# Cross-attention kernel: the first context, Wk, Wk_ip and x loads as one row on one DMA queue, in place of halves on two queues

## The chip, the cores and the metric

The kernel runs on one core of one Trainium2 chip. The metric is the device time of one execution in microseconds (us), the median of several runs. All data is float32.

## The reference, cut to what matters

`x` is (2, 2048, 640), `ctx_2048` is (2, 154, 1024). The 154 context rows are 77 text rows and 77 image rows, each with its own keys and values; there are 20 heads of 32.

```python
text, ip = ctx[:, :77], ctx[:, 77:]
q        = split_heads(x @ Wq.T)                       # 640 -> 20 heads x 32
k, v     = split_heads(text @ Wk.T), split_heads(text @ Wv.T)          # 1024 -> 640
k_ip, v_ip = split_heads(ip @ Wk_ip.T), split_heads(ip @ Wv_ip.T)
out = softmax(q k^T / sqrt(32)) v + softmax(q k_ip^T / sqrt(32)) v_ip
result = merge_heads(out) @ Wo.T + bo + x
```

## The kernel before, in words

All matrices lie transposed in HBM, the contracted dimension first. The 640 channels are cut into 5 chunks of 128 (`NC`), the 1024 context channels into 8 (`NCC`), and each batch's 2048 tokens into 4 blocks of 512 (`NHB`). A unit of work is a pair of a channel chunk (four heads) and half of the tokens; for each unit TensorE (PE) computes queries and scores, ScalarE (ACT), VectorE (DVE) and GpSimd (POOL) do the softmax, and PE applies it to the values. The order of everything behind the start is written out by hand in the string `SCHEDULE`; each engine works through its own instructions in that order. The change touches only what stands ahead of that string, the start of the program:

- Five small matmuls on zeros (line 576).
- The first queries, for chunks 0 of two units, from x's first block: lines 580 and 207. They need the five slices of x's first block (`xs[0]`, 128 channels by 512 tokens each; the first is loaded as two halves) and the first two column chunks of Wq (`wq_first`, which lies in the tile `aT`).
- The first two key projections, `project_kv(0)` (text, Wk) and `project_kv(1)` (image, Wk_ip), line 145. Each has eight steps, over the context chunks `k`. They need the context (`cT`, which lies in the tile `wo_ct`) and one 128-column slice of Wk and of Wk_ip (`load_w`, line 130; the slots lie in `aT`).
- Then `SCHEDULE` begins: the queries of x's second block (`q.0.1`, line 207, from `xs[1]`), the first scores (line 243), queries from x's third block, the first value projections (line 145 again, Wv and Wv_ip), and so on.

The transfers are issued from two queues: SyncE's (SP) and ScalarE's (ACT), `queues = nc.sync, nc.scalar`. ACT issues its transfers in line with its other work. Ahead of the loads that the change touches stand, split over both queues, x's first block and Wq's first two column chunks. Then, before:

```python
    for n, queue in enumerate(queues):
        load_ctx(n * half, queue)                       # context chunks 0-3 on SP, 4-7 on ACT
    for t in range(2):
        for n, queue in enumerate(queues):
            load_w(t, queue, slice(n * half, (n + 1) * half))   # Wk, then Wk_ip: rows of 0-3 on SP, 4-7 on ACT
    for k in range(NC):
        load_x(queues[k % 2])                           # x's second block: slices 0, 2, 4 on SP, 1, 3 on ACT
```

Behind these, all on SP: Wq's third column chunk (line 564), x's third block, Wv, Wv_ip, x's fourth block, the bias.

In the built program each transfer signals one of eight completion semaphores (DMAHW0 to DMAHW7), given out in turn over both queues together. A transfer is issued only when the transfer that last had its semaphore has landed, and the queue's later transfers wait behind it; so at most eight are under way.

Of the kernel before, what the change touches and what calls it, by code (L numbers as in the profile page):

```python
# [20 lines left out]
def kernel(  # L21
# [25 lines left out]
    nc = tc.nc  # L47
    P = 128
    NC = C // P
    NCC = CC // P  # L50
# [76 lines left out]
    wlist = [(src, c) for c in range(NC) for src in (WkT, WkipT, WvT, WvipT)]  # L127
    loaded = {}

    def load_w(n, queue=nc.sync, ks=slice(0, NCC)):  # L130

        src, c = wlist[n]
        w = wslots[n % len(wslots)]
        rows = src[ks.start * P : ks.stop * P, ts(c, P)]
        queue.dma_start(out=w[:, ks], in_=rows.rearrange("(k p) o -> p k o", p=P))
        loaded[n] = w

    def keys_in(ps):
# [33 lines left out]
    def load_x(queue=nc.sync):  # L172

        if slices:
            i, k = slices.pop(0)
            queue.dma_start(out=xs[i][:, k], in_=xT[ts(k, P), ts(i, TB)])
# [358 lines left out]
    queues = nc.sync, nc.scalar  # L535
    slices.pop(0)

    def load_first(queue, k, c, m=3):
        queue.dma_start(  # L539
            out=wq_first[:, k, c:m].rearrange("p c o -> p (c o)"), in_=WqT[ts(k, P), c * P : m * P]  # L540
        )

    half = NCC // 2

    def load_ctx(k, queue):
        queue.dma_start(
            out=wo_ct[:, ds(k * B * LT, half * B * LT)].rearrange("p (k n) -> p k n", k=half),
            in_=ctxT[ds(k * P, half * P), :].rearrange("(k p) n -> p k n", p=P),
        )
# [4 lines left out]
    for k in range(1, NC):  # L554
        load_x(queues[1 - k % 2])
        load_first(queues[k % 2], k, 0, 2)
    for n, queue in enumerate(queues):
        load_ctx(n * half, queue)
    for t in range(2):
        for n, queue in enumerate(queues):  # L560
            load_w(t, queue, slice(n * half, (n + 1) * half))
    for k in range(NC):
        load_x(queues[k % 2])
    nc.sync.dma_start(out=wq_first[:, :, 2], in_=WqT[:, ts(2, P)].rearrange("(k p) o -> p k o", p=P))
    for _ in range(NC):
        load_x()
    load_w(2)
    load_w(3)
    for _ in range(NC):
        load_x()  # L570
# [235 lines left out]
    for c, stages in enumerate(chains_of):  # L806
        for _, text in stages:
            for _, t in terms(text):
                for h in range(NH):
                    o = int(t[0]), NH * int(t[1]) + h  # L810
# [128 lines left out]
```

## Time and profile before

| | us |
|---|---|
| median of 3 runs | 496.41 (496.37 to 497.61) |
| profiled execution, its time | 499.75 |
| profiled execution, span from first to last instruction | 497.9 |
| PE busy in the span | 491.0 (99%) |
| DVE busy | 414.0 (83%) |
| POOL busy | 370.5 (74%) |
| ACT busy | 309.5 (62%) |

A profile is of one execution; its times count from the start of the span. In its rows "SPq" and "ACTq" are the instructions that issue transfers, q1 is SP's queue and q10 is ACT's. In a row of the timeline the first number is the start, the second the duration of all that the row merges, xN the number of instructions, and in brackets stands the idle time ahead of it and what ended it. A float32 matmul of the code shows as two PE instructions, so a key projection of eight steps is x16. PEclk is the share of the full TensorE clock that was granted. "Landing" is the time from a transfer's issue to its completion.

### The profile page before, as it was taken

To read this page: it belongs to the slowest core of one execution; us is meant where nothing else is said; L and a number is where in the kernel's file an instruction comes from. 1 tells how busy PE (TensorE), PEld (TensorE's weight loads), DVE (VectorE), ACT (ScalarE), POOL (GpSimd) and SP (SyncE) were. 2 spreads that over 40 slices of the span, in tenths; PEclk is the share of its full clock that TensorE was granted. 3 is DMA by queue.
4 is the path that set the end of the run, shared out by engine and by line. 5 is a ranking of instruction groups with operands and counts; after the bars stand their busy time and mean duration, and the time that the engine had idled before them with its cause. 6 is when DMAs were issued, how large, how long until landed. Compare 5 with 4: busy or idle time off the path is not lost.

```text
span 497.9 us, 10488 instructions
## 1 busy us (share of the span) xinstructions
PE 491.0 (99%) x4116; PEld 289.5 (58%) x4116; DVE 414.0 (83%) x416; ACT 309.5 (62%) x1002; POOL 370.5 (74%) x158
## 2 busy tenths in 40 slices
PE   9899999999999999999999999999999999999997
PEld 5666648548457547446566654754655685444443
DVE  0049999998899989979987996777789898999996
ACT  0266678978686778768899787577889862100000
POOL 0049988998988988978995768476589899798700
PEclk9899999999999999999999999999999999999999
DMA  8993044402341544696460667446551212320125
GB/s 285 302 311 90 10 130 116 130 2 74 82 149 44 168 135 132 211 393 198 113 223 18 182 213 240 136 142 204 187 145 42 87 45 85 128 84 2 42 84 211
DMA packets 67137, 69.38 MB, mean 139 GB/s; under 512 B 5520, under 2 KB 47120, under 8 KB 67088
## 3 DMA queue, kind: packets, MB, share of 16 engines
q1 hardware_dynamic: 64208, 65.86, 42.4%
q10 hardware_dynamic: 2880, 2.86, 1.8%
q8 instruction: 32, 0.52, 0.4%
q14 instruction: 17, 0.14, 0.1%
HBM read 54.94 MB, written 10.49 MB: 131 GB/s over the span
## 4 chain that ended last, share of the span: by engine, by line
PE 96%; DMA 3%; ACTq 0%; ACT 0%; DVE 0%; issue 0%; DVEq 0%
PE bank L207 34%; PE bank L890 11%; PE bank L342 11%; PE bank L243 10%; PE bank L500 10%; PE bank L145 9%; PE bank L481 7%; PE bank L510 3%; DMA aT<-in_L_xattn_Wk_dram 2%; DMA x<-in_x_dram 1%; ACTq L539 0%; ACT pb L255 0%; ACTq L553 0%; DVE acc L833 0%; DVEq L934 0%
## 5 line engine op out<-in xcount | busy, mean ns | idle before, releaser
L326 POOL TENSOR_TENSOR pb<-pb,rden 128x1848 f32<-128x1848 f32 (+1 forms) x60 | 176.0, 2943 | 30.4 <-DVE rden L321 23.9
L305 POOL TENSOR_TENSOR pb<-pb,mx 128x1848 f32<-128x1848 f32 (+1 forms) x39 | 121.5, 3128 | 58.7 <-DVE mx L291 58.5
L207 PE MATMUL bank<-x,wq 128*128 128x512 f32 x280 | 125.4, 598 | 0.1
L333 DVE STREAM_TRANSPOSE pb<-pb 128x1920 f32<-128x1920 f32 (+1 forms) x60 | 115.9, 1938 | 9.1 <-POOL pb L326 8.9
L291 DVE TENSOR_REDUCE mx<-pb 128x24 f32<-128x1848 f32 (+1 forms) x50 | 91.6, 1844 | 35.4 <-ACT pb L255 35.2
L255 ACT COPY pb<-bank 128x462 f32<-128x462 f32 (+1 forms) x200 | 85.4, 543 | 29.3 <-PE bank L243 28.9
L316 DVE TENSOR_REDUCE den<-pb 128x24 f32<-128x1848 f32 (+1 forms) x47 | 88.9, 1895 | 15.6 <-ACT pb L311 12.7
L207 PEld LDWEIGHTS bank<-x,wq 128*128 128x128 f32 x280 | 51.7, 190 | 60.0 <-issue 58.8
L311 ACT ACTIVATE pb<-pb 128x1848 f32<-128x1848 f32 (+1 forms) x39 | 65.6, 1684 | 17.5 <-POOL pb L305 17.4
L279 ACT ACTIVATE pb<-bank,mx 128x77 f32<-128x77 f32 x208 | 60.4, 388 | 6.5 <-DVE mx L294 6.5
L279 ACT ACTIVATE pb<-pb,mx 128x77 f32<-128x77 f32 x184 | 54.2, 355 | 1.9 <-DVE mx L291 1.8
L342 PE MATMUL bank<-pb,v 32*32 32x512 f32 x1600 | 55.2, 597 | 0.0
L207 PE MATMUL bank<-x,aT 128*128 128x512 f32 x116 | 52.0, 597 | 0.0
L145 PE MATMUL bank<-wo_ct,aT 128*128 128x154 f32 x320 | 47.4, 303 | 2.1 <-DMA aT<-in_L_xattn_Wk_dram 2.1
L243 PEld LDWEIGHTS bank<-kT,qT 32*128 32x128 f32 x1024 | 36.1, 184 | 21.6 <-issue 13.2
L145 PEld LDWEIGHTS bank<-wo_ct,aT 128*128 128x128 f32 x320 | 44.7, 194 | 5.8 <-issue 5.1
L243 PE MATMUL bank<-kT,qT 32*128 32x154 f32 x1024 | 45.1, 305 | 0.0
L279 ACT ACTIVATION_READ_ACCUMULATOR pb<-bank,mx 128x1 f32 x168 | 44.1, 268 | 0.0
L342 PEld LDWEIGHTS bank<-pb,v 32*32 32x32 f32 x1600 | 28.9, 103 | 22.7 <-issue 10.1
L481 PE MATMUL bank<-aT,wo_ct 128*128 128x512 f32 x80 | 36.3, 595 | 0.0
L207 PEld LDWEIGHTS bank<-x,aT 128*128 128x128 f32 x116 | 21.4, 191 | 24.1 <-issue 23.7
L500 PE MATMUL bank<-aT,wo_ct 128*128 128x256 f32 x128 | 32.2, 386 | 0.0
(83 smaller groups left out, 511.9 us busy)
## 6 DMA issues: line engine op xcount, KB each, us to landing
x<-in_x_dram SPq DMA_DIRECT2D x20, 1280.0 KB, 7.0
out_dram<-acc SPq DMA_DIRECT2D x19, 256.0 KB, 2.6
acc<-in_x_dram SPq DMA_DIRECT2D x16, 256.0 KB, 5.0
x<-in_x_dram SPq DMA_DIRECT2D x15, 256.0 KB, 5.7
out_dram<-x SPq DMA_DIRECT2D x15, 256.0 KB, 2.1
v<-vS SPq DMA_DIRECT2D x160, 20.0 KB, 2.9
aT<-in_L_xattn_Wv_dram SPq DMA_DIRECT2D x5, 512.0 KB, 5.7
aT<-in_L_xattn_Wv_ip_dram SPq DMA_DIRECT2D x5, 512.0 KB, 4.2
```

Source lines behind the costliest of these rows:

```text
L145: nc.tensor.matmul(keys_in(out), loaded[n][:, k, :], cT[:, k, :, t, :], start=(k == 0), stop=(k == NCC - 1))
L207: nc.tensor.matmul(pq, weight_of(q)[:, k, :], xs[place_of(u, h)][:, k, :], start=(k == 0), stop=(k == NC - 1), skip_group_check=loose,)
L243: nc.tensor.matmul(ps[g][:, ts(t, 2 * L)], qTs[(u, h)][g * D : (g + 1) * D, ts(st, P)], kT[g * D : (g + 1) * D, c, b].rearrange("p t l -> ...
L255: nc.scalar.copy(keys_of(u, s)[:, :, g], ps[g][:, : n * 2 * L].rearrange("p (n l) -> p n l", n=n))
L279: nc.scalar.activation(row, row if ps is None else rows_in(ps[g], n)[:, t, x], AF.Exp, bias=maxs[(u, s)][:, *one], accum_out=None if den i ...
L291: nc.vector.tensor_reduce(mx, rows_of(u, s), AX.X, ALU.max, negate=negate)
L305: nc.gpsimd.tensor_tensor(rows_of(u, s), rows_of(u, s), maxs[(u, s)].unsqueeze(3).to_broadcast([P, n, 2, L]), ALU.subtract)
L316: nc.vector.tensor_reduce(den_of(u, s), rows_of(u, s), AX.X, ALU.add)
L326: nc.gpsimd.tensor_tensor(rows_of(u, s), rows_of(u, s), rdens[(u, s)].unsqueeze(3).to_broadcast([P, n, 2, L]), ALU.mult)
L333: nc.vector.transpose(p, p)
L342: nc.tensor.matmul(pa[r][g * D : (g + 1) * D, :], v4s[q % 2][rows, g, k, :], zones[rows, :, g, k, :], start=(k == 0), stop=(k == NK - 1),)
L500: nc.tensor.matmul(part, w_of[m][:, kp, op], t_of(m, b, i)[:, kp], start=(op == kp == 0 and m in (1, 2, 5)), stop=(op == 1 and kp == 1 and ...
```

## The change

The context still comes in two halves, but Wk and Wk_ip come whole, and all of these and the five slices of x's second block are issued by SP, in this order: context chunks 0-3, Wk, context chunks 4-7, Wk_ip, x slices 0 to 4. ACT issues nothing behind x's first block and Wq. What is computed, and the order of it on PE, DVE and POOL, is the same.

```diff
-    def load_w(n, queue=nc.sync, ks=slice(0, NCC)):
+    def load_w(n):
 
         src, c = wlist[n]
         w = wslots[n % len(wslots)]
-        rows = src[ks.start * P : ks.stop * P, ts(c, P)]
-        queue.dma_start(out=w[:, ks], in_=rows.rearrange("(k p) o -> p k o", p=P))
+        nc.sync.dma_start(out=w, in_=src[:, ts(c, P)].rearrange("(k p) o -> p k o", p=P))
         loaded[n] = w
...
-    def load_ctx(k, queue):
-        queue.dma_start(
+    def load_ctx(k):
+        nc.sync.dma_start(
...
-    for n, queue in enumerate(queues):
-        load_ctx(n * half, queue)
-    for t in range(2):
-        for n, queue in enumerate(queues):
-            load_w(t, queue, slice(n * half, (n + 1) * half))
-    for k in range(NC):
-        load_x(queues[k % 2])
+    for k in (0, half):
+        load_ctx(k)
+        load_w(k // half)
+    for _ in range(NC):
+        load_x()
     nc.sync.dma_start(out=wq_first[:, :, 2], in_=WqT[:, ts(2, P)].rearrange("(k p) o -> p k o", p=P))
```

SP, behind its part of x's first block and Wq, before (`wo_ct` holds the context, `aT` the weights, `x_83` is x's second block):

```order
L546 DMA wo_ct<-in_ctx_dram 128x4x308 [waits DMAHW3_49]
L135 DMA aT<-in_L_xattn_Wk_dram 128x4x128 [waits DMAHW5_49]
L135 DMA aT<-in_L_xattn_Wk_ip_dram 128x4x128 [waits DMAHW7_49]
L176 DMA x_83<-in_x_dram 128x512 [waits DMAHW1_49]
L176 DMA x_83<-in_x_dram 128x512 [waits DMAHW3_49]
L176 DMA x_83<-in_x_dram 128x512 [waits DMAHW5_49]
L564 DMA aT<-in_L_xattn_Wq_dram 128x5x128 [waits DMAHW6_49]
```

SP at the same place in the changed kernel (its line numbers are up to three lower):

```order
L545 DMA wo_ct<-in_ctx_dram 128x4x308 [waits DMAHW3_49]
L134 DMA aT<-in_L_xattn_Wk_dram 128x8x128 [waits DMAHW4_49]
L545 DMA wo_ct<-in_ctx_dram 128x4x308 [waits DMAHW5_49]
L134 DMA aT<-in_L_xattn_Wk_ip_dram 128x8x128 [waits DMAHW6_49]
L175 DMA x_83<-in_x_dram 128x512 [waits DMAHW7_49]
L175 DMA x_83<-in_x_dram 128x512 [waits DMAHW0_49]
L175 DMA x_83<-in_x_dram 128x512 [waits DMAHW1_49]
L175 DMA x_83<-in_x_dram 128x512 [waits DMAHW2_49]
L175 DMA x_83<-in_x_dram 128x512 [waits DMAHW3_49]
L561 DMA aT<-in_L_xattn_Wq_dram 128x5x128 [waits DMAHW4_49]
```

Wk's transfer now reuses semaphore 4, which Wq's second slice had on ACT, and Wq's third column chunk reuses that of Wk itself, where it reused that of ACT's half of Wk.

ACT from its last transfer of x's first block on, before:

```order
L176 DMA x_82<-in_x_dram 128x512 [waits DMAHW2_49]
L546 DMA wo_ct<-in_ctx_dram 128x4x308 [waits DMAHW4_49]
L135 DMA aT<-in_L_xattn_Wk_dram 128x4x128 [waits DMAHW6_49]
L135 DMA aT<-in_L_xattn_Wk_ip_dram 128x4x128 [waits DMAHW0_49]
L176 DMA x_83<-in_x_dram 128x512 [waits DMAHW2_49]
L176 DMA x_83<-in_x_dram 128x512 [waits DMAHW4_49]
L221 ACT_TABLE_LOAD
L221 ACTIVATE qT_0_153<-bank_71 128x512 [waits PE_49]
L221 ACTIVATE aT<-bank_72 128x512 [waits PE_49]
```

And in the changed kernel:

```order
L175 DMA x_82<-in_x_dram 128x512 [waits DMAHW2_49]
L220 ACT_TABLE_LOAD
L220 ACTIVATE qT_0_151<-bank_71 128x512 [waits PE_49]
L220 ACTIVATE aT<-bank_72 128x512 [waits PE_49]
L590 COPY kT<-bank_69 128x77 [waits PE_49]
```

Five transfers leave ACT, and the load of its function table follows directly on x's first block.

PE at the two key projections and the start of `q.0.1`, before:

```order
L145 MATMUL bank_69<-wo_ct,aT 128x154 [waits DMAHW5_49,DMAHW3_49]
L145 MATMUL bank_69<-wo_ct,aT 128x154 x3
L145 MATMUL bank_69<-wo_ct,aT 128x154 [waits DMAHW6_49,DMAHW4_49]
L145 MATMUL bank_74<-wo_ct,aT 128x154 [waits DMAHW7_49]
L145 MATMUL bank_74<-wo_ct,aT 128x154 [waits DMAHW0_49]
L207 MATMUL bank_72<-x_83,aT 128x512 [waits DMAHW1_49,Activation_49]
```

And in the changed kernel:

```order
L144 MATMUL bank_69<-wo_ct,aT 128x154 [waits DMAHW4_49,DMAHW3_49]
L144 MATMUL bank_69<-wo_ct,aT 128x154 x3
L144 MATMUL bank_69<-wo_ct,aT 128x154 [waits DMAHW5_49]
L144 MATMUL bank_74<-wo_ct,aT 128x154 [waits DMAHW6_49]
L144 MATMUL bank_74<-wo_ct,aT 128x154 x7
L206 MATMUL bank_72<-x_83,aT 128x512 [waits DMAHW7_49,Activation_49]
```

PE's work is the same; the first step of each projection now waits for the whole of its weights, the fifth step of the first one for the second half of the context alone.

## Prediction

> **What bounds the kernel now.** First the page: shares, the slices of the span, the chain of waits.
>
> ```profile
> span 497.9 us, 10488 instructions
> ...
> PE 491.0 (99%) x4116; PEld 289.5 (58%) x4116; DVE 414.0 (83%) x416; ACT 309.5 (62%) x1002; POOL 370.5 (74%) x158
> ...
> PEclk9899999999999999999999999999999999999999
> ...
> PE 96%; DMA 3%; ACTq 0%; ACT 0%; DVE 0%; issue 0%; DVEq 0%
> ```
>
> PE is busy for 99% of the span and is 96% of the chain that ends it. The only other share of weight is DMA's 3%, and the only slices in which PE's clock is below nine tenths lie at the start (the second digit, 12 to 25 us). So I read the chain's first 40 us in order of time (start, duration, what):
>
> ```profile
> 2.14 5.79 DMA x<-in_x_dram
> ...
> 7.95 9.53 DMA aT<-in_L_xattn_Wk_dram
> ...
> 17.61 5.06 PE bank L145 x24
> 22.67 4.29 PE bank L207 x10
> ...
> 28.75 4.49 PE bank L207 x10
> ...
> 33.97 4.41 PE bank L145 x32
> ```
>
> and PE's own timeline at that place, and the granted clock around it (stretch, then length, busy time of PE, PEld, DVE, ACT and POOL, then PEclk, DMA share, GB/s):
>
> ```profile
> 14.34 1.22 PE L145 MATMUL bank<-wo_ct,aT 128*128 128x154 f32 x8
> 17.61 5.06 PE L145 MATMUL bank<-wo_ct,aT 128*128 128x154 f32 x24 [2.06 <-DMA aT<-in_L_xattn_Wk_dram]
> ```
> ```profile
> 14.50:17.50 3.00, 1.05 (x8) 0.82 (x7) 0.00 (x0) 2.08 (x3) 0.00 (x0) 1.00 1.11 354
> 17.50:18.00 0.50, 0.39 (x2) 0.42 (x3) 0.00 (x0) 0.29 (x1) 0.00 (x0) 0.79 0.98 353
> 18.00:21.00 3.00, 3.00 (x14) 3.00 (x13) 0.00 (x0) 0.35 (x2) 0.00 (x0) 0.50 0.85 264
> 21.00:21.50 0.50, 0.50 (x5) 0.50 (x4) 0.00 (x0) 0.00 (x0) 0.00 (x0) 0.80 0.80 143
> ```
>
> PE does four steps of the first key projection (8 instructions), then stands 2.06 us until ACT's half of Wk, issued at 7.95, lands at 7.95 + 9.53 = 17.48. Behind the wait it runs at half clock: 0.21 of the 0.5 us to 18.0, all 3.0 us to 21.0, 0.2 us after that, 3.41 us in all. PE's list of waits (us, times, longest) has nothing else but its start, so what it loses here moves everything behind it:
>
> ```profile
> PE bank L145 <- DMA aT<-in_L_xattn_Wk_dram: 2.1, 1, 2.1
> PE bank L576 <- DVE pb L574: 1.0, 1, 1.0
> ```
>
> **The change part by part.** *The stall and its clock.* The 24 instructions behind the wait took 5.06 us; the 32 of the first value projections take 4.41, so 24 at full clock are 24 x 4.41/32 = 3.31 us. The slow clock costs 5.06 - 3.31 = 1.75 us (half of 3.41 us of half clock is 1.71, the same). Stall and clock together are 2.06 + 1.75 = **3.81 us**; that is what there is to gain. The Trainium skill's TensorE: Matmul & The Clock Gate (What's actually happening) lets the clock fall after an idle window of about 3.4 us; by that rule a 2.06 us stall would cost itself alone, and the sum would be 2.06. The row says 0.50 behind a stall of 2.06, so the measurement decides, and I keep 1.75.
>
> *Why Wk is late.* These are issues on ACT, from its last slice of x's first block on, with its table load and its second copy of queries, and on SP:
>
> ```profile
> 5.20 0.33 ACTq L176 DMA_DIRECT2D x<-in_x_dram  x1
> 7.15 0.39 ACTq L546 DMA_DIRECT2D wo_ct<-in_ctx_dram  x1
> 7.95 0.38 ACTq L135 DMA_DIRECT2D aT<-in_L_xattn_Wk_dram  x1
> 8.67 0.43 ACTq L135 DMA_DIRECT2D aT<-in_L_xattn_Wk_ip_dram  x1
> ...
> 15.41 1.28 ACT L221 ACT_TABLE_LOAD   x1 [15.41 <-DMA aT<-in_L_xattn_Wk_dram]
> ...
> 17.20 0.59 ACT L221 ACTIVATE aT<-bank 128x512 f32<-128x512 f32 x1
> ```
> ```profile
> 5.00 0.39 SPq L546 DMA_DIRECT2D wo_ct<-in_ctx_dram  x1
> ...
> 8.30 4.46 SPq L176 DMA_DIRECT2D x<-in_x_dram  x3
> 17.49 0.38 SPq L564 DMA_DIRECT2D aT<-in_L_xattn_Wq_dram  x1
> ...
> 21.07 0.63 SPq L135 DMA_DIRECT2D aT<-in_L_xattn_Wv_ip_dram  x1
> ```
>
> While ACT's Wk waits its turn, SP's slices of x's second block, not needed before 22.67, move. From 16.0 to 17.5 us, the last stretch before the landing, the queues carried (packets, MB):
>
> ```profile
> q1 hardware_dynamic: 245, 0.45, 83.2%
> q10 hardware_dynamic: 90, 0.12, 22.5%
> ```
>
> 0.45 MB of x on q1 against 0.12 MB of weights on q10. The change puts x behind both weights on one queue. Whether that suffices is a sum of bytes.
>
> *When the loads land.* In MB: x's first block and Wq's two chunks are 1280 + 640 KB = 1.97, a half of the context 0.63, Wk 0.52, Wk_ip 0.52, a slice of x 0.26. In a row they end at 2.60 (context, first half), 3.12 (Wk), 3.75 (second half), 4.28 (Wk_ip), 4.54 (x's slice 0), 5.59 (slice 4). Up to 9.0 us the trace moved (and up to 28.0, for the lag below):
>
> ```profile
> DMA packets 1917, 2.37 MB, mean 263 GB/s; under 512 B 171, under 2 KB 1421, under 8 KB 1917
> ```
> ```profile
> DMA packets 8848, 8.28 MB, mean 296 GB/s; under 512 B 470, under 2 KB 7029, under 8 KB 8848
> ```
>
> Up to there both kernels move almost the same. For the rates I take windows of the trace, the second of them mostly Wv and Wv_ip, which have Wk's form, on SP's queue alone, the third x alone:
>
> ```profile
> 9.00:13.00 4.00, 4.00 (x10) 1.71 (x9) 0.00 (x0) 0.00 (x0) 0.00 (x0) 1.00 1.11 339
> 25.50:27.50 2.00, 2.00 (x20) 0.99 (x22) 0.00 (x0) 0.50 (x1) 0.00 (x0) 1.00 1.21 302
> 28.50:30.00 1.50, 1.50 (x11) 0.69 (x6) 0.10 (x1) 1.50 (x5) 0.00 (x0) 1.00 1.03 370
> ```
>
> Context at 339 GB/s, weights at 302, x at 370: the context's first half is through at 9.0 + 0.23/0.339 = 9.7, Wk at 11.4, the second half at 13.3, Wk_ip at 15.0, x's slices from 15.7 to 18.5. A landing comes later than the bytes:
>
> ```profile
> wo_ct<-in_ctx_dram SPq DMA_DIRECT2D x1, 616.0 KB, 6.6
> ...
> aT<-in_L_xattn_Wv_ip_dram SPq DMA_DIRECT2D x1, 512.0 KB, 8.2
> ```
>
> The context half issued at 5.00 landed at 11.6, its last byte being the 2.60th MB, moved at 9.7: 1.9 us. Wv_ip, issued at 21.07, landed at 29.3; all that stands ahead of it and itself are 8.27 MB, moved at 28.0: 1.3 us. With 1.3 to 1.9 the landings are Wk 12.7 to 13.3, context's second half 14.6 to 15.2, **Wk_ip 16.3 to 16.9**, x's slices 17.0 to 17.6 and then up to 20.4.
>
> *When PE wants them.* It comes to the first projection at 14.34 as now, to its fifth step at 14.34 + 8 x 0.138 = 15.44, to Wk_ip at 16.55, to x's second block at 18.75 and to its last slice 3.4 us later. Wk has 1.0 us to spare or more, the context 0.2 or more, x over 1.1. Wk_ip is a draw: PE waits for 0 to 0.4 us. I take 0.2, the middle, and no slow clock for it: the only stall of the trace with the clock recorded behind it is ten times as long. Gain 3.81 - 0.2 = 3.6; the ends are 3.8 and, with a wait of 0.4, 3.4.
>
> *What else moves.* SP issues nine transfers where it had six, three more at some 0.43 us; at 9.0 there are 4.28 - 2.37 = 1.9 MB queued ahead of the first x slice, and Wq's third chunk, held until 17.49 by ACT's half of Wk, now waits for Wk alone, 13 or so. Wk itself is issued at 7.15, when Wq's second slice on ACT lands (ACT's context half waits for the same there), 2.5 us before its first byte is due; without that cover each 0.4 us would count in full. SP can also be held behind two 512 KB loads:
>
> ```profile
> L176 SPq DMA_DIRECT2D x<-in_x_dram x5: 430/430/3990, 21.8 to 27.2; - x5
> ```
>
> An x slice right behind Wv and Wv_ip took 3.99 us to issue. The same at 8.4 ends at 12.4, still 2.6 us before its bytes are due. Loads for later (x's third block, due at 28.75 - 3.8) start no later than now, since SP stood from 12.8 to 17.49 there. ACT's table load moves from 15.41 to the time after its last issue at 5.2, and the copies of the first queries with it; PE needs the bank they free at 18.75, and at 17.8, where the second copy ends now, it would be in time. Worth nothing while the 4.4 us of projections cover it. DVE, POOL and ACT start their softmax from PE's scores and shift with it.
>
> **The rivals.** *The stall stays, at Wk_ip.* All loads use the same engines, and the last weights may land hardly earlier. Before, ACT's half of Wk_ip landed at 18.8:
>
> ```profile
> aT<-in_L_xattn_Wk_ip_dram ACTq DMA_DIRECT2D x1, 256.0 KB, 10.1
> ```
>
> If Wk_ip keeps 18.8, PE waits 18.8 - 16.55 = 2.2 us and pays the slow clock again, 1.75: 496.6. If it lands 1 us late and the clock falls, 3.81 - 2.75 = 1.1 us remain: 495.3. For it: the margin is nil. Against it: 0.45 MB of x went ahead of it from 16.0 to 17.5 alone. The Trainium skill's DMA: Bandwidth & Descriptors (Rules for kernel authors) has it that spreading transfers over issuing engines, or splitting one in two, gains nothing since all run on the same 16 engines; the rates above agree, and by that rule alone the change would be worth nothing, as in this rival's first case. It leaves the order of the bytes out.
>
> *The stall is smaller outside the profile.* The profiled execution took 499.75 us, 3.3 more than the median of 496.41, and its span of 497.9 alone is longer than the median. If part of that excess is this stall, the plain runs hold less of it: with none of it they stay at 496.4, with the stall of 2.06 alone and no slow clock they gain 2 (494.4); the middle is 495.4. Against it: an excess can lie anywhere.
>
> *Slower: one queue at a time does not keep the engines full.* There is a stretch with SP's queue alone at
>
> ```profile
> 20.50:22.50 2.00, 2.00 (x14) 2.00 (x13) 0.00 (x0) 0.00 (x0) 0.00 (x0) 0.83 0.86 204
> ```
>
> At r GB/s from 9.0 on, Wk_ip's 1.91 MB end at 9.0 + 1910/r and land 1.4 later; the gain is gone when PE waits 2.1 us there (plus 1.75 of clock), landing at 18.6: r = 233. At 204 it lands at 19.8, PE waits 3.2 + 1.75, 1.1 more than now: 497.5. Below 197 it is slower by over 0.3%; at 174, midway between this row and the 143 of its worst half us above, it lands at 21.4 and loses 4.8 + 1.75 - 3.81 = 2.7: 499.1. Against it: the other windows of SP's queue alone hold 302 and 370.
>
> **How the numbers follow.** The sum is against the profiled execution: 499.75 - 3.6 = 496.2, span 494.3. The median is 3.3 below that time, so for plain runs I take the same 3.6 off: 496.41 - 3.6 = **492.8**. A measurement of this kernel can tell about 0.3%, 1.5 us, from no change. Chances: forecast 0.70 (492.2 to 494), stall at Wk_ip 0.12 (0.05 of it faster by 0.3%, 0.07 within), smaller stall outside the profile 0.09 (0.04 and 0.05), slower 0.09. Faster 0.79, same 0.12, slower 0.09. The range, 491.9 to 496.0, takes in both bounds of the forecast, the rivals' better cases, and leaves out the slower one and the first rival's worse end.
>
> **What would show it.** Right: no PE wait of 2 us at line 144, a clock of 1.00 from 14 to 22 us, `q.0.1` at 18.7 to 19.2 instead of 22.67, Wq's third chunk issued near 13, and the whole later timeline 3.4 to 3.8 us earlier. Wrong: a wait of over 0.5 us at the first projections with half clock behind it; q1 below 240 GB/s between 9 and 15 us; or `q.0.1` early and PE waiting later for x's third block or Wv, so that the end does not move.

## The result, and the profile after

| | kernel before | changed kernel |
|---|---|---|
| median of 20 runs, us | 497.46 (496.23 to 499.37) | 496.10 (495.41 to 496.47) |
| profiled execution, us | 499.75 | 496.36 |
| its span, us | 497.9 | 494.6 |

The ratio is 0.9976, 95% interval 0.9969 to 0.9983: faster by 0.24%, some 1.2 us. That is a third of the forecast 3.6 (the medians themselves differ by 1.36), and the median stands 0.1 us above the range. The median of 496.41 from which the forecast was counted came from three runs; over twenty, with those three among them, it is 497.46.

The page of the changed kernel has PE's clock at nine tenths or more in every slice:

```profile
span 494.6 us, 10484 instructions
...
PE 489.1 (99%) x4116; PEld 287.7 (58%) x4116; DVE 413.9 (84%) x416; ACT 309.5 (63%) x1002; POOL 370.5 (75%) x158
...
PEclk9999999999999999999999999999999999999999
```

The chain at its start in order of time, where the kernel before had Wk's second half (7.95, 9.53) and 24 instructions in 5.06 us:

```profile
7.71 9.24 DMA aT<-in_L_xattn_Wk_ip_dram
...
17.00 2.37 PE bank L144 x16
19.37 4.29 PE bank L206 x10
...
30.67 4.41 PE bank L144 x32
```

PE's timeline at the two key projections, with its waits in brackets, and the last row `q.0.1`:

```profile
13.75 1.22 PE L144 MATMUL bank<-wo_ct,aT 128*128 128x154 f32 x8
15.23 1.32 PE L144 MATMUL bank<-wo_ct,aT 128*128 128x154 f32 x8 [0.27 <-DMA wo_ct<-in_ctx_dram]
17.00 2.37 PE L144 MATMUL bank<-wo_ct,aT 128*128 128x154 f32 x16 [0.44 <-DMA aT<-in_L_xattn_Wk_ip_dram]
19.21 4.45 PE L206 MATMUL bank<-x,aT 128*128 128x512 f32 x10
```

Two small waits, 0.71 us together, have taken the place of one of 2.06. The granted clock in the stretches that were at 0.50 and 0.80 before:

```profile
18.00:21.00 3.00, 3.00 (x16) 2.04 (x15) 0.00 (x0) 0.35 (x2) 0.00 (x0) 1.00 1.10 351
21.00:21.50 0.50, 0.50 (x3) 0.26 (x2) 0.00 (x0) 0.00 (x0) 0.00 (x0) 1.00 1.07 389
```

`q.0.1` starts at 19.21 instead of 22.51: 3.30 us earlier, and the two spans differ by 3.3. So between these two executions the prediction's sum is nearly right. What does not fit is the medians: the execution of before that was profiled, 499.75 us, is above all of its twenty runs.

### The profile page after: what moved, and what is told of

The parts are those of the page before. It is cut to its first block, busy times and chain, and to the rows that moved or that the text cites. A ratio compares the mean times of both kernels' runs of the same rounds, so it can differ in the third digit from the quotient of the medians.

```text
span 494.6 us, 10484 instructions
## 1 busy us (share of the span) xinstructions
PE 489.1 (99%) x4116; PEld 287.7 (58%) x4116; DVE 413.9 (84%) x416; ACT 309.5 (63%) x1002; POOL 370.5 (75%) x158
## 4 chain that ended last, share of the span: by engine, by line
PE 96%; DMA 3%; ACTq 0%; ACT 0%; DVE 0%; DVEq 0%; issue 0%
PE bank L206 34%; PE bank L887 12%; PE bank L341 11%; PE bank L242 11%; PE bank L499 10%; PE bank L144 9%; PE bank L480 7%; PE bank L509 3%; DMA aT<-in_L_xattn_Wk_ip_dram 2%; DMA x<-in_x_dram 1%; ACTq L538 0%; ACT pb L254 0%; ACTq L552 0%; DVE acc L830 0%; DVEq L931 0%
## 5 line engine op out<-in xcount | busy, mean ns | idle before, releaser
L144 PE MATMUL bank<-wo_ct,aT 128*128 128x154 f32 x320 | 46.0, 297 | 0.7 <-DMA aT<-in_L_xattn_Wk_ip_dram 0.4
L144 PEld LDWEIGHTS bank<-wo_ct,aT 128*128 128x128 f32 x320 | 43.0, 188 | 4.7 <-issue 3.0
L220 ACT ACTIVATE qT<-bank 128x512 f32<-128x512 f32 x32 | 19.3, 631 | 23.4 <-PE bank L206 23.4
```

The lines of the kernel that those rows point to most:

```text
L144: nc.tensor.matmul(keys_in(out), loaded[n][:, k, :], cT[:, k, :, t, :], start=(k == 0), stop=(k == NCC - 1))
```

## The experiments

A profile and the mean clock of every run came with each kernel; the intervals are against runs of the kernel before in the same chip session, whose medians were 497.37 to 497.49. The profiled execution is one of the runs.

**The kernel before, again** (no edit).

> The kernel before, unchanged, to see one more profile of it and the clock of each of its runs. Theory A: every run has the wait for the second half of Wk, but half clock behind it follows in some runs only; then the runs fall in two groups, mean clock 0.997 and 1.000, about 1.7 us apart (near 499 and near 497), and most runs are in the second. Theory B: the wait itself is about 1 to 2 us shorter in most runs, and the clock falls where it is long; then spans vary without the clock, and this profile shows a PE wait well below 2.06 us. Theory C: the profile of before was typical, and the profiling cost plain runs 3.3 us less; then this profile again shows 2.06 us and 3.4 us of half clock, while the runs beside it are near 497.4.

Measured: median 497.30, 0.9997 [0.9987, 1.0008]. The new profile has a shorter wait and no half clock behind it; PE's timeline and two stretches behind the wait:

```profile
14.26 1.22 PE L145 MATMUL bank<-wo_ct,aT 128*128 128x154 f32 x8
17.00 3.40 PE L145 MATMUL bank<-wo_ct,aT 128*128 128x154 f32 x24 [1.52 <-DMA aT<-in_L_xattn_Wk_dram]
20.24 4.45 PE L207 MATMUL bank<-x,aT 128*128 128x512 f32 x10
```
```profile
17.00:18.00 1.00, 1.00 (x7) 1.00 (x8) 0.00 (x0) 0.23 (x1) 0.00 (x0) 1.00 1.03 374
18.00:19.00 1.00, 1.00 (x10) 1.00 (x9) 0.00 (x0) 0.35 (x2) 0.00 (x0) 1.00 0.95 294
```

The 24 instructions take 3.40 us, not 5.06. C falls: this profiled execution, 497.48 us, lies in the middle of the runs beside it, and in all runs the time is 1.7 to 1.9 us above the span. A and B both hold in part: half clock is in some runs only, and the wait is shorter here. Over all experiments 81 further runs of this kernel show a clock: 4 have 0.997 and take 499.72 to 500.40 us, the other 77 take 496.05 to 498.55. So half clock of the length of the first profile's is there in about one run of twenty (three of the 77 show 0.998, at 497.40 to 497.56 us), and the rest still vary by 2.5 us.

**Two more profiles of the kernel before** (no edit).

> The kernel before once more, for one more profile. If the half clock of the first profile was chance, this one shows a PE wait between 1.0 and 2.1 us at the first key projection and a clock of 1.00 behind it, with a time of 496.3 to 498.3. If it is the rule, 0.50 shows again.

> As the run ahead of it, a fourth profile of the kernel before: the wait between 1.0 and 2.1 us, clock 1.00 behind it, and the second-block queries starting near 20.2 to 20.9 us.

Measured: 497.43 and 497.20 us, `q.0.1` at 20.15 and 19.93. The start of `q.0.1` is near what I said (the second lies 0.27 us ahead of it), the reason is not: neither profile lists a wait for Wk. The timeline of the first of the two:

```profile
4.13 3.78 PE L580 MATMUL bank<-x,aT 128*128 128x256 f32 x8 [0.58 <-DMA aT<-in_L_xattn_Wq_dram]
7.71 8.12 PE L207 MATMUL bank<-x,aT 128*128 128x512 f32 x16
15.67 4.64 PE L145 MATMUL bank<-wo_ct,aT 128*128 128x154 f32 x32
20.15 4.45 PE L207 MATMUL bank<-x,aT 128*128 128x512 f32 x10
```

PE comes to the first projection at 15.67 instead of 14.34, and Wk's second half, which held Wq's third chunk until 16.79 here, is in time for the fifth step, or late by 0.26 us at most: the 32 instructions take 4.64 us here and 4.38 in the second of the two profiles, where PE comes at 15.71. The first queries took 8.12 us where the first profile of before has 7.24. Their weight loads show why; first this kernel's, then the first profile's of before:

```profile
8.56 0.34 PEld L207 LDWEIGHTS bank<-x,aT 128*128 128x128 f32 x1 [0.52 <-issue]
9.42 0.34 PEld L207 LDWEIGHTS bank<-x,aT 128*128 128x128 f32 x1 [0.52 <-issue]
10.09 0.19 PEld L207 LDWEIGHTS bank<-x,aT 128*128 128x128 f32 x1 [0.34 <-issue]
10.52 0.19 PEld L207 LDWEIGHTS bank<-x,aT 128*128 128x128 f32 x1 [0.24 <-issue]
```
```profile
7.23 0.43 PEld L207 LDWEIGHTS bank<-x,aT 128*128 128x128 f32 x2 [0.53 <-issue]
7.90 0.19 PEld L207 LDWEIGHTS bank<-x,aT 128*128 128x128 f32 x1 [0.24 <-issue]
8.33 0.19 PEld L207 LDWEIGHTS bank<-x,aT 128*128 128x128 f32 x1 [0.24 <-issue]
```

At the start PE runs at half rate (a load of 0.34 us every 0.86) and changes to full rate (0.19 every 0.43) near 7.3 us in one execution and near 9.9 in another. The clock column does not show it; in this kernel's profile it reads 1.00 (the third number from the end) ahead of the change as well as behind it:

```profile
8.50:9.00 0.50, 0.50 (x2) 0.34 (x1) 0.00 (x0) 0.00 (x0) 0.00 (x0) 1.00 1.02 355
10.50:11.00 0.50, 0.50 (x3) 0.24 (x2) 0.00 (x0) 0.00 (x0) 0.00 (x0) 1.00 1.09 341
```

So in some executions of before PE waits for Wk, and in others Wk does not matter, since PE is late itself.

**The changed kernel, again** (no edit).

> The changed kernel once more, for a second profile of it: waits of 0 to 1 us at the first projections, full clock, and the second-block queries starting at 18.8 to 19.5 us, so 1.0 to 1.6 us ahead of the usual start of the kernel before.

Measured: 497.01 us, outside its own twenty runs. PE came late here too, at 14.66, and Wk_ip was later still:

```profile
14.66 2.50 PE L144 MATMUL bank<-wo_ct,aT 128*128 128x154 f32 x16
17.60 2.38 PE L144 MATMUL bank<-wo_ct,aT 128*128 128x154 f32 x16 [0.44 <-DMA aT<-in_L_xattn_Wk_ip_dram]
19.82 4.45 PE L206 MATMUL bank<-x,aT 128*128 128x512 f32 x10
```

`q.0.1` at 19.82 is behind the expected 18.8 to 19.5. With it there are four profiles of before and two of the change, and in all six the time less the start of `q.0.1` is nearly the same: 499.75 - 22.51, 497.48 - 20.24, 497.43 - 20.15 and 497.20 - 19.93 give 477.24 to 477.28; 496.36 - 19.21 and 497.01 - 19.82 give 477.15 and 477.19. What lies behind the start of `q.0.1` takes the same in both kernels to 0.13 us, and all but that of the effect is when `q.0.1` starts. Read back from the medians, that is 497.46 - 477.26 = 20.2 us before and 496.10 - 477.17 = 18.9 after.

**All halves on one queue.**

```diff
-    for n, queue in enumerate(queues):
-        load_ctx(n * half, queue)
-    for t in range(2):
-        for n, queue in enumerate(queues):
-            load_w(t, queue, slice(n * half, (n + 1) * half))
-    for k in range(NC):
-        load_x(queues[k % 2])
+    for n in range(2):
+        load_ctx(n * half, nc.sync)
+        load_w(0, nc.sync, slice(n * half, (n + 1) * half))
+    for n in range(2):
+        load_w(1, nc.sync, slice(n * half, (n + 1) * half))
+    for k in range(NC):
+        load_x()
```

> Halves as before, but all on SP: context 0-3, Wk 0-3, context 4-7, Wk 4-7, Wk_ip 0-3, Wk_ip 4-7, then x. If the gain of the change is the single row (x behind the weights), this is as fast as the changed kernel (496.1, 0.997 to 0.998 of before), and where the changed kernel waits 0.44 us for the whole Wk_ip this waits only for its first half, which is through 0.87 us earlier, so it gains up to 0.4 us more (495.7). If whole transfers matter, it is slower than the changed kernel by about 1 us.

Measured: 495.77 us, 0.9973 [0.9962, 0.9983], the same as the changed kernel within the interval. Its timeline has no wait at the projections:

```profile
14.67 4.38 PE L145 MATMUL bank<-wo_ct,aT 128*128 128x154 f32 x32
18.89 4.45 PE L207 MATMUL bank<-x,aT 128*128 128x512 f32 x10
```

So the gain comes with the single row; whether the weights come whole or in halves makes no difference that these runs can tell.

**x's second block behind ACT's halves.**

```diff
     for k in range(NC):
-        load_x(queues[k % 2])
+        load_x(nc.scalar)
```

> The kernel before with one thing changed: all five slices of x's second block on ACT's queue, behind its halves of Wk and Wk_ip. Theory x-in-front: Wk's second half is late because SP's x slices overtake it; then it lands at 15.5 to 16.5 us instead of 17.48, PE waits 0 to 1 us without half clock, and the time is that of the changed kernel (496.1 to 496.6). Theory ACT-late: ACT's half is late because ACT issues it late and its queue lags behind; then the wait stays near 2 us and the time at that of before (497.4).

Measured: 499.80 us, 1.0053 [1.0035, 1.0071]: neither. In its profile no wait for Wk is listed (32 projection instructions in 4.79 us, 0.4 more than without any wait), but PE came late there, at 15.42. Another wait has come: ACT's table load and copies of the first queries, queued behind the five issues. ACT's rows, and PE's at `q.0.1`:

```profile
11.07 8.12 ACTq L176 DMA_DIRECT2D x<-in_x_dram  x5
...
19.22 1.28 ACT L221 ACT_TABLE_LOAD   x1 [19.22 <-DMA x<-in_x_dram]
...
21.01 0.59 ACT L221 ACTIVATE aT<-bank 128x512 f32<-128x512 f32 x1
```
```profile
21.65 4.56 PE L207 MATMUL bank<-x,aT 128*128 128x512 f32 x10 [1.44 <-ACT aT L221]
```

I had not counted what stands behind those issues on ACT. The run does not decide between the two theories. Of its six runs two have a clock of 0.997 (500.74 and 501.52), four of 1.000 (498.92 to 499.91).

**x's second block cut to 16 columns.**

```diff
     nc.gpsimd.memset(vT[:, :, 2 * L :], 0.0)
+    nc.gpsimd.memset(xs[1].rearrange("p k t -> p (k t)"), 0.0)
...
         if slices:
             i, k = slices.pop(0)
+            if i == 1:
+                queue.dma_start(out=xs[i][:, k, :16], in_=xT[ts(k, P), ds(i * TB, 16)])
+                return
             queue.dma_start(out=xs[i][:, k], in_=xT[ts(k, P), ts(i, TB)])
```

> The kernel before with x's second block cut to 16 of 512 columns in each of its five transfers (the rest of that tile is set to zero on POOL, idle then, and its queries are computed on that); queues, order and semaphores stay. Theory x-in-front: the 0.45 MB of x that overtake ACT's half of Wk are gone, so it lands about 0.45/0.38 = 1.2 us earlier, near 16.0 us instead of 16.9 to 17.5, PE waits 0.3 to 0.6 us there and the time is near that of the changed kernel, 496.0 to 496.4. Theory ACT-late: the landing stays at 16.9 or later and the time at 497.3.

This kernel leaves out most of x's second block, so its results there are not those of the others. Measured: 496.45 us, 0.9976 [0.9958, 0.9994]: the time of the changed kernel, with the loads on two queues as before. Wq's third chunk, which waits for ACT's half of Wk, was issued at

```profile
15.26 0.38 SPq L568 DMA_DIRECT2D aT<-in_L_xattn_Wq_dram  x1
```

in its profile, against 17.49, 16.88, 16.79 and 15.76 in those of before. From ACT's issue to its landing this half of Wk took 7.6 us, against 9.5, 8.3, 9.0 and 8.3. PE has no wait listed, and its 32 projection instructions took 4.67 us, so it lost at most 0.3. The profiled execution took 495.88 us and has `q.0.1` at 18.61; the difference, 477.27, is that of the other profiles, so the missing bytes gain nothing later on. So with x's bytes out of the way, two queues do as well as one row: what the theory of x in front says, and not what that of ACT being late says. The interval is wide, the landing is from one profile, and the earliest one of before is only 0.5 us later.

**A long wait made on purpose.**

```diff
     for k in (0, half):
         load_ctx(k)
-        load_w(k // half)
+        if k == 0:
+            load_w(0)
     for _ in range(NC):
         load_x()
+    load_w(1)
```

> The changed kernel with Wk_ip issued behind x's second block instead of ahead of it, which makes a long wait on purpose: 1.3 MB of x at 370 GB/s are 3.5 us more ahead of Wk_ip, so it lands near 20.4 instead of 16.95 and PE waits near 4 us. If half clock follows every wait of that length, all runs show a mean clock near 0.996 to 0.997 and the time is 496.1 + 3.5 + 1.7 = 501.3, in one group. If half clock depends on where the wait falls, runs fall in two groups, near 499.6 and 501.3.

Measured: 500.87 us, 1.0061 [1.0041, 1.0082]; a wait of 3.83 us, and two groups: 498.78 and 498.92 at a clock of 1.000, 500.71 to 501.81 at 0.993 to 0.996. The profile is one of the second:

```profile
20.07 4.04 PE L144 MATMUL bank<-wo_ct,aT 128*128 128x154 f32 x16 [3.83 <-DMA aT<-in_L_xattn_Wk_ip_dram]
```

16 instructions take 4.04 us here and 2.37 in the changed kernel. By the clocks, half clock follows in four runs of six, though the wait is made near 3.8 us long (it was measured in the profiled one alone); it costs some 2 us where it does.

**Seven matmuls on zeros at the start instead of five**, in the kernel before, the changed one and the row of halves.

```diff
-    for _ in range(5):
+    for _ in range(7):
```

> The kernel before with seven instead of five matmuls on zeros at the start, so that PE does not stand between them (they end at 3.55) and the first queries (3.6 to 4.3). Theory start-clock: in the profiles of before the weight loads of the first queries go from 0.34 to 0.19 us at 7.3 us in two and at 9.9 in two; where it is late PE reaches the first key projection at 15.7 instead of 14.3 and finds Wk landed, so the loads are not what it waits for. With PE never idle the full clock comes earlier (4.5 to 7.9), PE reaches the projection near 13.5 to 14.5 in every run, always waits for Wk (1.5 to 3 us), and more runs show half clock behind it: median 497 to 498.5, no better than before. Rival: the start clock has no part in it; then 497.4 plus the 0.5 us of more matmuls or less.

> The changed kernel with seven instead of five matmuls on zeros. Theory start-clock: PE reaches the first projection near 13.5 to 14.5 in every run and then waits for loads, Wk_ip at 17.0 to 17.6 above all; median 495.5 to 496.1, and the lead over the kernel before with seven matmuls is 1.5 to 2.5 us, more than the 1.4 us with five. Rival: the lead stays 1.4 us or shrinks.

> The single row of halves (no PE wait in its profile, the second-block queries at 18.9) with seven matmuls on zeros. Theory start-clock: only PE's arrival limits it, so an earlier full clock is worth most here: median 494.8 to 495.5, below both kernels. Rival: 495.8 as with five.

Measured: before 497.73, 1.001 [0.9993, 1.0028]; changed 495.72, 0.997 [0.9956, 0.9985]; halves 495.80, 0.9969 [0.9955, 0.9983]. The lead of the change is now 2.0 us, as expected, but these intervals do not separate it from the 1.4 with five. The half clock that I expected in more runs of before is in one of twelve (0.997, 500.31 us). PE's arrival at the first projection, in the profiles of the first two:

```profile
13.79 1.29 PE L145 MATMUL bank<-wo_ct,aT 128*128 128x154 f32 x8 [0.37 <-DMA aT<-in_L_xattn_Wk_dram]
16.10 3.40 PE L145 MATMUL bank<-wo_ct,aT 128*128 128x154 f32 x24 [1.02 <-DMA aT<-in_L_xattn_Wk_dram]
19.34 4.45 PE L207 MATMUL bank<-x,aT 128*128 128x512 f32 x10
```
```profile
14.11 4.38 PE L144 MATMUL bank<-wo_ct,aT 128*128 128x154 f32 x32
18.33 4.45 PE L206 MATMUL bank<-x,aT 128*128 128x512 f32 x10
```

In these two PE comes at about the same time; the kernel before then waits 1.39 us for Wk, the changed one not at all, though I had expected it to wait for Wk_ip. The profile of before is of the fastest of its twelve runs, 496.59 us; its median, read back as above, puts `q.0.1` at 20.5, no earlier than with five matmuls. The halves do not gain the extra expected of them: in their profile, of the slowest of their twelve runs (496.75), a wait of 0.7 us for Wk has come back, and 0.6 for ACT stands behind `q.0.1`. Changed and halves are 0.08 us apart, and neither differs from its time with five matmuls (496.10 and 495.77) by more than these runs can tell.

## Why the prediction was wrong

- **The step that failed** is "Stall and clock together are 2.06 + 1.75 = 3.81 us; that is what there is to gain", carried to the plain runs with "for plain runs I take the same 3.6 off". The row was right and the execution was not typical. Half clock was taken for a part of every run though it came from one execution, and so was a wait that depends on when PE arrives. The 1.75 us of half clock are in 4 of 81 runs, and the 2.06 us of waiting were 1.52 in one other profile and nothing, or 0.26 at most, in two, where PE itself came at 15.7. The start of `q.0.1` that was to be moved is 22.51 in that profile, 19.9 to 20.2 in the three others. Read back from the medians it moved from 20.2 to 18.9: 1.3 us, where the sum has 3.6.
- **The sign of it was in the text**: the profiled execution stood 3.3 us above the median, nearly the whole of the term. The second rival, a smaller stall outside the profile, said so, got 0.09, and is what happened. Profiling did not add the excess, as every run takes 1.7 to 1.9 us more than its span, the profiled one too; the profiled execution was itself a long one.
- **PE's arrival** was taken as 14.34 "as now", a constant. It is 13.75 to 15.71 over the six profiles of the two kernels, with the moment at which PE goes from half to full rate and with when the first slices land. Where PE is late, the change has no wait to remove.
- **Landings**: Wk at 6.45 + 7.0 = 13.5, the context's second half at 6.87 + 8.3 = 15.2, Wk_ip at 16.95, x's first slice at 9.16 + 8.5 = 17.7 were all at the late end of the ranges or up to 0.2 us past it. PE came to Wk_ip at 15.23 + 1.32 = 16.55, as said, and waited 0.44 us where 0 to 0.4 was said. The other wait, 0.27 us for the context, which I had cleared with 0.2 to spare, comes from PE and not from the landing, which is in its range: PE started at 13.75, 0.6 us ahead of the 14.34 that the sum had.
- **Right**: Wk_ip is the load that decides next; no half clock behind a wait that short; SP is held behind two 512 KB loads and nothing pays for it; ACT's move is worth nothing; no later wait takes the gain back (time less start of `q.0.1` is the same in both kernels to 0.13 us). `q.0.1` at 19.21 is what was said. Wq's third chunk at 14.46 is 1.5 us later than said, since SP was busy with its five issues of x until 9.16 + 5.25 = 14.41. Of the rivals, the first did not show: Wk_ip landed at 16.95 and not at 18.8. Nor did the slower one: the loads moved at 330 GB/s from 9 to 13 us.
- **The range** missed by 0.1 us since it was counted from a three-run median 1.05 us too low. That is not what failed: counted from 497.46, the same sum gives 493.9, still 2.2 us below the measured median, and the forecast gain is three times the measured one.

These rows carry the landings and the rate:

```profile
wo_ct<-in_ctx_dram SPq DMA_DIRECT2D x1, 616.0 KB, 8.3
aT<-in_L_xattn_Wk_dram SPq DMA_DIRECT2D x1, 512.0 KB, 7.0
```
```profile
6.45 0.37 SPq L134 DMA_DIRECT2D aT<-in_L_xattn_Wk_dram  x1
6.87 0.64 SPq L545 DMA_DIRECT2D wo_ct<-in_ctx_dram  x1
...
9.16 5.25 SPq L175 DMA_DIRECT2D x<-in_x_dram  x5
14.46 0.43 SPq L561 DMA_DIRECT2D aT<-in_L_xattn_Wq_dram  x1
```
```profile
9.00:13.00 4.00, 4.00 (x11) 1.82 (x10) 0.00 (x0) 0.00 (x0) 0.00 (x0) 1.00 1.06 330
```

Not settled: in what share of runs PE's start is late, since each run but the profiled ones gives only its time and clock, and what sets the moment of full rate. With seven matmuls the loads were at 0.19 us by 6.8 to 7.7 in the three profiles taken, too few to say that it always comes so early.

Nor is it settled how the 1.3 us of the medians divide between a wait that is gone and an earlier PE. From PE's arrival to `q.0.1` it takes 4.22 us without any wait (15.71 to 19.93). The slowest of the changed kernel's twenty runs, 496.47 us, puts `q.0.1` at 19.3 and so PE's arrival at 15.1 at the latest. An arrival near 15.7, as in two of the four profiles of before, is in none of those twenty, and no run here says why.

## What to carry to other kernels

When the profiled execution is slower than the median by about as much as the term that is to be removed, look first whether the term is in the usual execution at all: a second profile, and the clock of the plain runs, would have told it. A wait for a load is the difference of two moving times, the load's and the engine's arrival, and removing it gains only in those executions in which the load is the later. Here the loads needed late did best behind the loads needed first, on one queue, and did harm on an engine that had its own work queued behind the issues.

## What the runs showed of the hardware that was not expected

- Half clock behind a wait is a matter of chance here: it followed a wait of 2.06 us in one execution, none followed one of 1.52, and in the kernel with a wait made near 3.8 us long it followed in four runs of six. Behind the wait of 2.06 us it lasted 3.41 us.
- At the start PE ran at half rate to 7.3 us or to 9.9 us in executions of one kernel, and the clock column read 1.00 all the while; the weight loads, 0.34 against 0.19 us, show it.
